# Attention beside a scan: score and value products as separate steps, the negated maxima turned by one product and carried to their rows by DMA

## Chip, core and metric

The kernel runs on one core of a Trainium2 chip. The metric is the device time of one execution in microseconds (us); for the kernel before it is the median of three runs. A profile is one more execution, recorded by the hardware; it gives every instruction's engine, line, start and duration. The engines: PE (TensorE, matrix products; PEld its weight loads), DVE (VectorE), ACT (ScalarE), POOL (GpSimd), SP (SyncE, which issues the DMAs). [...]

## What is computed

An input x of 16 images, 256 channels, 32 × 32 positions, float32, goes through two layers, each added to its own input. Layer 0 is attention over the 1024 positions of an image (4 heads of 32), layer 1 a selective state-space scan along the same 1024 positions (512 channels with 64 states each). Cut to what matters here:

```python
# layer 0, after group norm, position embedding and layer norm
q, k, v = (qkv[:, :, 0], qkv[:, :, 1], qkv[:, :, 2])
dots = jnp.einsum('bihd,bjhd->bhij', q, k) * scale
attn = jax.nn.softmax(dots, axis=-1)
out = jnp.einsum('bhij,bjhd->bihd', attn, v)
...
# layer 1
dA = jnp.exp(d_t[..., None] * A)
h = dA * h + (d_t * u_t)[..., None] * B_t[:, None, :]
y = jnp.einsum('bdn,bn->bd', h, C_t)
```

## The kernel before

**The scan sets the frame.** 512 channels × 64 states × 1024 positions of an image are cut into 256 *units*: 2 halves in time (t), 4 blocks of 128 channels (k), 4 quarters (q), 8 pairs of tiles (i). A unit is two tiles of 128 × 512. In the main loop (L927) each unit n does, in this order:

- `load(n + 6)` (L814): SP issues a DMA of 512 KB, the tile `dub`; there are seven buffers, so it waits until the scan of unit n − 1 has read its own;
- `inputs(n + 4)` (L824): POOL multiplies that tile twice in place;
- `scan(n)` (L846): DVE runs two scans over `dub` and the decays `a`;
- `decay(n + 2)`: PE makes two tiles `a` in PSUM (L833; four buffers, freed by `scan(n)`), ACT takes the exponential of each (L836);
- the *side work*: steps of another image's other stages, see below;
- a step of `outputs` (L870): the products of the states with C. A block of eight units has four halves of 16 output products on PE (L883), in the phases n mod 8 = 0, 1, 3, 4; after the second and fourth, ACT copies the sum away (`y`, L891) and in phases 2 and 5 PE turns it (L895); then ACT copies `yo` (L903) and SP stores it in phase 6 (L909).

**Side work is metered.** While the units of image b run, the other stages of image b + 1 (normalization, attention, the scan's inputs) and the last one of image b − 1 (gate and store) are produced by Python generators. Each `yield w` ends a step and says its weight w. Before the run, the weights of one image are summed; the loop (L951) adds `rate` per unit to `due` and takes steps until `due` is spent. So the steps of an image are spread over its units by weight, and a step's instructions stand in each engine's queue between `decay(n + 2)` and the `outputs` of that unit. At the end (L978) the program order is fixed by hand for PE, ACT, DVE and POOL; SP's queue follows the order of issue closely.

The first image's attention runs ahead of the first scan, the other fifteen beside the scans of the image before. The last image's scans have no attention beside them.

**Attention** (`attention_layer`, L324) takes two heads at a time, a *pair*, e = 0, 1 within it:

- `query_key(pair)` (L355): four steps; products into PSUM, then ACT copies 32 rows each to `qa` and `ka`. The head e has partitions 64e to 64e + 31; partition 64e + 32 of `ka` is set to ones by a small DMA (L358), and that of `qa` will take the negated maximum, so that one product of 33 rows gives score minus maximum;
- maxima: 16 steps (weight 1.1) of two score products each (L400), reduced by DVE in the next step (L391);
- rows: DVE negates the maxima into `neg`, with positions on partitions (L405). To bring them into one row, PE multiplies each of 16 columns by the identity (L412), a row of 128 each, and ACT copies four rows of 512 into `qa` (L415); two steps of 1.2;
- values: for each half of 512 query positions, eight steps of weight 1.5. Step j makes the two scores of key block j (L436), the value products of block j − 1 (L424), and the exponentials of j (L444), which free the two score buffers. One more step multiplies the last block and evacuates: ACT copies `ao` and `sums` of a head from the one PSUM accumulator `av` (L381, L382); the other head's copies follow in the next half's first step, or in a step of their own after the second half.

PSUM for all side work is a pool of two buffers (`mm`, L92).

Of the kernel before, what the change touches and what calls it, by code (L numbers as in the profile page):

```python
# [11 lines left out]
F32 = mybir.dt.float32  # L12
BF16 = mybir.dt.bfloat16
AF = mybir.ActivationFunctionType
# [5 lines left out]
P = 128  # L20
# [3 lines left out]
HL = 512  # L24
# [3 lines left out]
NJ = L // P  # L28
DI = 512
ND = DI // P  # L30
NS = 64
# [17 lines left out]
NV = _n  # L49
# [3 lines left out]
def attention_then_scan_kernel(  # L53
# [18 lines left out]
    nc = tc.nc  # L72
# [5 lines left out]
    const = pool("const", 1)  # L78
# [3 lines left out]
    ptp = pool("ptp", 4)  # L82
    small = pool("small", 2)
# [10 lines left out]
    def psum(name, dims=P):  # L94
        return mm.tile([P, HL], F32, name=name, tag="mm")[:dims]
# [7 lines left out]
    def hs(h):  # L103
        return ts(h, HL)


    vec = const.tile([P, NV], F32, name="vec")
    nc.sync.dma_start(vec, vecs)

    def col(name, i=0, n=1):  # L110
        o, w = _COLS[name]
        assert i + n <= w
        return vec[:, o + i : o + i + n]
# [5 lines left out]
    ident = const.tile([P, P], F32, name="ident")  # L119
# [13 lines left out]


    a_neg = work("a_neg", ND * NS)
    nc.scalar.activation(a_neg, col("A_log", 0, ND * NS), AF.Exp)
    nc.vector.tensor_scalar(a_neg, a_neg, -1.0, None, ALU.mult)
    acol = const.tile([P, DI // 2], F32, name="acol")
    a2 = work("a2", 2 * P).rearrange("p (j n i) -> p j n i", j=2, i=2)
    for k in range(ND):  # L140
# [4 lines left out]
        for j in range(2):  # L145
# [3 lines left out]
                start=(j == 0), stop=(j == 1),  # L149
# [22 lines left out]
    t = work("ones_s")[:1]  # L172
# [151 lines left out]
    def attention_layer(b):  # L324
# [54 lines left out]
        def evacuate(pair, hf, e):  # L379
            h, o = 2 * pair + e, 2 * DH * e  # L380
            nc.scalar.copy(ao[ts(h, DH), hs(hf)], av[o : o + DH])  # L381
            nc.scalar.copy(sums[ts(h, DH), hs(hf)], av[o + DH : o + 2 * DH])  # L382

        for pair in range(HEADS // 2):
            qa, ka = yield from query_key(pair)
            mx = small.tile([P, 2, NJ, 2], F32, name="mx", tag="mx")
            waiting = []

            def maxima():
                for s, e, c, hf in waiting:  # L390
                    nc.vector.tensor_reduce(mx[:, e, c, hf : hf + 1], s, AX.X, ALU.max)  # L391
                waiting.clear()

            for c in range(NJ):
                for hf in range(2):
                    maxima()
                    for e in range(2):
                        r = ds(2 * DH * e, DH)
                        s = psum("s_ps")
                        nc.tensor.matmul(s, qa[r, ts(c, P)], ka[r, hs(hf)], start=True, stop=True)  # L400
                        waiting.append((s, e, c, hf))
                    yield 1.1
            maxima()
            neg = small.tile([P, 2, NJ], F32, name="neg", tag="neg")
            nc.vector.tensor_reduce(neg, mx, AX.X, ALU.max, negate=True)  # L405
            for e in range(2):
                o = 2 * DH * e + DH
                for hf in range(2):
                    row = psum("row_ps", 1)
                    for c in range(NJ // 2):  # L410
                        i = hf * (NJ // 2) + c
                        nc.tensor.matmul(  # L412
                            row[:, ts(c, P)], neg[:, e, i : i + 1], ident, start=True, stop=True
                        )
                    nc.scalar.copy(qa[o : o + 1, hs(hf)], row)  # L415
                yield 1.2
            if pair == 0:
                ao, sums = work("ao"), work("sums")
            for hf in range(2):
                pts = []  # L420

                def values(j):
                    for e in range(2):
                        nc.tensor.matmul(  # L424
                            av[ts(e, 2 * DH)],
                            vv[j // (NJ // 2)][:, j % (NJ // 2), 2 * pair + e, :], pts[e],
                            start=(j == 0), stop=(j == NJ - 1),
                        )
                    pts.clear()

                for j in range(NJ):
                    scores = []
                    for e in range(2):
                        r = ds(2 * DH * e, DH + 1)
                        s = psum("st_ps")
                        nc.tensor.matmul(s, ka[r, ts(j, P)], qa[r, hs(hf)], start=True, stop=True)  # L436
                        scores.append(s)
                    if j == 1:
                        av = accp.tile([P, HL], F32, name="av", tag="av")
                    if pts:  # L440
                        values(j - 1)
                    for s in scores:
                        pt = ptp.tile([P, HL], F32, name="pt", tag="pt")
                        nc.scalar.activation(pt, s, AF.Exp)  # L444
                        pts.append(pt)
                    if j == 0 and hf == 1:
                        evacuate(pair, 0, 1)
                    yield 1.5
                values(NJ - 1)
                evacuate(pair, hf, 0)  # L450
                yield 1
            evacuate(pair, 1, 1)
            yield 1
# [584 lines left out]
```

## Time and profile before

| what | value |
|---|---|
| median of 3 runs | 13837.73 us |
| lowest and highest run | 13811.08 and 13840.92 us |
| the profiled execution | 13864.42 us |
| its span, first to last instruction | 13862.6 us |
| mean granted TensorE clock | 0.727 |
| DMA | 2804.18 MB, mean 202 GB/s |
| one scan (L846), 128 × 512 | 1203 ns in an image's first half, 1263 ns in its second |
| one product of a tile on POOL (L824) | 1302 ns |
| one exponential of the decay (L836) | 660 ns |
| one exponential of scores (L444) | 608 ns |
| one copy of a row of 512 (L415) | 573 ns, 128 of them |
| one instruction of the row products (L412) | 336 ns, 1024 of them |

How to read it: the page gives busy time by engine, then groups of instructions with their mean duration and the idle time before them. Float32 products appear as two instructions each, and their ends are modelled, so their durations overlap: the distance between starts is the better measure of what PE needs. A stretch of the run can be taken alone: "windows" list, for a stretch given by its start and end, its length, then busy time and count for PE, PEld, DVE, ACT and POOL, then the granted clock, the DMA engines' busy share and GB/s. "Timeline" lists instructions in order of time (start, length, engine, line, operation, tiles, count), with the idle time before one in brackets.

### The profile page before, as it was taken

Reading aid. Unit: us, or ns where it says so; the run is one execution under the profiler, and the core shown is the slowest. Engines: PE = TensorE matmul, PEld = TensorE weight load, DVE = VectorE, ACT = ScalarE, POOL = GpSimd, SP = SyncE. Lnnn points to the kernel's source line nnn. Section 1 sums busy time; section 2 is a strip of 40 time slices with the busy share of each in tenths; the row PEclk is TensorE's granted clock in tenths of the full one; section 3 lists DMA queues with packets and bytes.
Section 4 is the critical chain, followed back from the end, with each engine's and each line's share of the span. In section 5 each row is a group of like instructions: output and inputs, shape, how many; then the busy total and the mean of one; then the engine's idle time right before and its main releaser. Section 6 shows DMA issues by size and latency. Waiting matters only on the chain. (4 is left out here: it accounts for less than half of the span.)

```text
span 13862.6 us, 435096 instructions
## 1 busy us (share of the span) xinstructions
PE 11218.2 (81%) x185744; PEld 5762.9 (42%) x185744; DVE 12145.4 (88%) x11699; ACT 8103.3 (58%) x14245; POOL 10462.1 (75%) x8214
## 2 busy tenths in 40 slices
PE   7787977879788797887878878797787978879767
PEld 2344444444444444443444444444444444444434
DVE  2799888898989889888898888989898898988999
ACT  2565665656655566555665656566565665556544
POOL 0588777777787777777777777777777778777788
PEclk6776777767778677786777767677676777767767
DMA  1466566565665656656566665656666566565666
GB/s 38 166 207 226 187 201 220 197 229 182 204 221 196 229 179 214 211 197 224 194 210 206 201 217 199 220 193 202 220 200 228 185 206 223 193 230 183 213 215 225
DMA packets 964174, 2804.18 MB, mean 202 GB/s; under 512 B 138162, under 2 KB 285747, under 8 KB 962228
## 3 DMA queue, kind: packets, MB, share of 16 engines
q1 hardware_dynamic: 962228, 2776.34, 59.9%
q8 instruction: 1452, 23.79, 0.7%
q14 instruction: 494, 4.05, 0.1%
HBM read 2514.18 MB, written 261.62 MB: 200 GB/s over the span
## 5 line engine op out<-in xcount | busy, mean ns | idle before, releaser
L824 POOL TENSOR_TENSOR dub<-dub,bt 128x512 f32<-128x512 f32 x8192 | 10407.0, 1302 | 3350.8 <-DMA dub<-dus 2960.7
L836 ACT ACTIVATE a<-a,acol 128x512 f32<-128x512 f32 x8192 | 5066.9, 660 | 3844.0 <-PE a L833 3808.6
L846 DVE TENSOR_TENSOR_SCAN h<-a,last,dub 128x512 f32<-128x512 f32 x4096 | 4939.7, 1263 | 246.6 <-POOL dub L824 188.3
L846 DVE TENSOR_TENSOR_SCAN h<-a,dub 128x512 f32<-128x512 f32 x4096 | 4705.0, 1203 | 286.8 <-POOL dub L824 150.6
L833 PE MATMUL a<-pieces,pick 48*128 48x512 bf16 x8192 | 2915.2, 481 | 2261.8 <-DVE h L846 2215.0
L883 PEld LDWEIGHTS yb<-h,cd 128*32 128x32 f32 x131072 | 2685.0, 140 | 1992.8 <-issue 1725.0
L883 PE MATMUL yb<-h,cd 128*32 128x64 f32 x131072 | 3093.9, 266 | 26.1 <-issue 14.2
L833 PEld LDWEIGHTS <-pick 48*128 48x128 bf16 x8192 | 506.6, 96 | 2632.6 <-issue 2418.5
L400 PE MATMUL s_ps<-ka,qa 32*128 32x512 f32 x2048 | 1142.4, 1025 | 42.0 <-ACT ka L371 26.4
L391 DVE TENSOR_REDUCE mx<-s_ps 128x1 f32<-128x512 f32 x1024 | 656.9, 680 | 302.7 <-PE s_ps L400 301.3
L895 PEld LDWEIGHTS yb<-turn,y 128*16 128x16 f32 x32768 | 416.5, 120 | 1028.2 <-ACT y L891 409.0
L891 ACT COPY y<-yb 128x256 f32<-128x256 f32 x1024 | 383.7, 375 | 765.4 <-PE yb L883 762.9
L895 PE MATMUL yb<-turn,y 128*16 128x32 f32 x32768 | 552.3, 216 | 149.4 <-ACT y L891 139.2
L436 PE MATMUL st_ps<-qa,ka 33*128 33x512 f32 x2048 | 634.9, 654 | 2.6 <-ACT pt L444 2.5
L424 PE MATMUL av<-pt,vv 128*64 128x512 f32 x2048 | 613.0, 678 | 0.9
L444 ACT ACTIVATE pt<-st_ps 128x512 f32<-128x512 f32 x1024 | 559.3, 608 | 77.1 <-PE st_ps L436 75.5
L400 PEld LDWEIGHTS s_ps<-ka,qa 32*128 32x128 f32 x2048 | 350.1, 277 | 429.7 <-DVE mx L391 237.2
L618 PE MATMUL g_ps<-w,xp 128*128 128x256 f32 x1536 | 453.6, 451 | 0.0
L618 PEld LDWEIGHTS g_ps<-w,xp 128*128 128x128 f32 x1536 | 391.1, 328 | 102.5 <-issue 63.3
L603 DVE SCALAR_TENSOR_TENSOR u<-up,cwh,u 128x1024 f32<-128x1024 f32 x192 | 304.4, 1585 | 27.4 <-ACT u L595 27.1
L771 PE MATMUL m_ps<-w,xs 128*128 128x256 f32 x1024 | 316.2, 458 | 10.5 <-DVE xs L746 10.5
L771 PEld LDWEIGHTS m_ps<-w,xs 128*128 128x128 f32 x1024 | 261.3, 328 | 90.2 <-issue 59.4
(135 smaller groups left out, 7581.0 us busy)
## 6 DMA issues: line engine op xcount, KB each, us to landing
dub<-dus SPq DMA_DIRECT2D x4096, 512.0 KB
dps<-pc SPq DMA_DIRECT2D x384, 128.0 KB
pieces<-dps SPq DMA_DIRECT2D x1024, 48.0 KB
xs<-in_x_dram SPq DMA_DIRECT2D x64, 512.0 KB
xs<-kept SPq DMA_DIRECT2D x64, 512.0 KB
zs<-z SPq DMA_DIRECT2D x64, 512.0 KB
ud<-u SPq DMA_DIRECT2D x64, 512.0 KB
dus<-du SPq DMA_DIRECT2D x64, 512.0 KB
```

The source lines that it names most:

```text
L391: nc.vector.tensor_reduce(mx[:, e, c, hf : hf + 1], s, AX.X, ALU.max)
L400: nc.tensor.matmul(s, qa[r, ts(c, P)], ka[r, hs(hf)], start=True, stop=True)
L424: nc.tensor.matmul(av[ts(e, 2 * DH)], vv[j // (NJ // 2)][:, j % (NJ // 2), 2 * pair + e, :], pts[e], start=(j == 0), stop=(j == NJ - 1),)
L436: nc.tensor.matmul(s, ka[r, ts(j, P)], qa[r, hs(hf)], start=True, stop=True)
L618: nc.tensor.matmul(ps[:, ts(q, C)], xp[k][:, ds(first + t, P, 4)], wg_s[:, k, t, :], start=(i == 0), stop=False,)
L771: nc.tensor.matmul(ps[:, ts(q, C)], us[d][:, ds(first, P, 4)], wo_s[:, d, :], start=(d == 0), stop=(d == ND - 1),)
L824: nc.gpsimd.tensor_tensor(v, v, blocks[b, t]["bt"], ALU.mult)
L833: nc.tensor.matmul(a, w, pieces[r], start=True, stop=True)
L836: nc.scalar.activation(a, a, AF.Exp, scale=acol[:, at : at + 1])
L846: nc.vector.tensor_tensor_scan(now["h", q % 2][:, 2 * i + e, :], decays[n][e], loaded[n][:, e, :], first, ALU.mult, ALU.add,)
L883: nc.tensor.matmul(yb[ts(g, 32), ts(s, 64)], cd[:, at // 16, ts(c, 32)], hbuf[:, :, at : at + 4], start=(c == 0), stop=(c == 3),)
L895: nc.tensor.matmul(out4[32 * s : 32 * s + 16, half, e], y2[:, 64 * s + e : 64 * s + 64 : 4], turn[:, e], start=True, stop=True,)
```

## The change

Inside attention:

- `query_key(0)` is made ahead of the loop over pairs, and `query_key(1)` in pair 0 after its rows, in place of the start of pair 1. In pair 1 two steps without instructions stand there.
- The 16 row products of a pair become one: `neg` with its 16 columns is the stationary operand, the identity moves; the result has 16 rows of 128. ACT copies it to a small tile `few`, 16 × 128, in one instruction. SP then issues two DMAs, each of which takes eight rows of 128 to the one row of 1024 in `qa`.
- A values step of 1.5 becomes a score step of 0.8 (two score products and their two exponentials) and a values step of 0.8 (the value products of the block before). Order on each engine is as before, scores of j ahead of values of j − 1.
- The weights of an image's attention fall from 112.8 to 112.0.
- To make room for `few`, the last columns of the vector constants (A_log) are no longer kept; they are fetched by a DMA of their own into a work tile at the start.

```diff
-    vec = const.tile([P, NV], F32, name="vec")
-    nc.sync.dma_start(vec, vecs)
+    NC = NV - ND * NS
+    vec = const.tile([P, NC], F32, name="vec")
+    nc.sync.dma_start(vec, vecs[:, :NC])
...
     a_neg = work("a_neg", ND * NS)
-    nc.scalar.activation(a_neg, col("A_log", 0, ND * NS), AF.Exp)
+    nc.sync.dma_start(a_neg, vecs[:, NC:])
+    nc.scalar.activation(a_neg, a_neg, AF.Exp)
...
+        ahead = yield from query_key(0)
         for pair in range(HEADS // 2):
-            qa, ka = yield from query_key(pair)
+            qa, ka = ahead
...
             nc.vector.tensor_reduce(neg, mx, AX.X, ALU.max, negate=True)
+            turned = psum("row_ps", 2 * NJ)[:, :P]
+            nc.tensor.matmul(
+                turned, neg.rearrange("p e c -> p (e c)"), ident, start=True, stop=True
+            )
+            few = small.tile([2 * NJ, P], F32, name="rows", tag="rows")
+            nc.scalar.copy(few, turned)
+            yield 1
             for e in range(2):
                 o = 2 * DH * e + DH
-                for hf in range(2):
-                    row = psum("row_ps", 1)
-                    for c in range(NJ // 2):
-                        i = hf * (NJ // 2) + c
-                        nc.tensor.matmul(
-                            row[:, ts(c, P)], neg[:, e, i : i + 1], ident, start=True, stop=True
-                        )
-                    nc.scalar.copy(qa[o : o + 1, hs(hf)], row)
-                yield 1.2
+                nc.sync.dma_start(
+                    qa[o : o + 1].rearrange("p (c t) -> p c t", c=NJ), few[ts(e, NJ)]
+                )
+            if pair == 0:
+                ahead = yield from query_key(1)
+            else:
+                yield 1
+                yield 1
...
                 for j in range(NJ):
-                    scores = []
+                    made = []
                     for e in range(2):
                         r = ds(2 * DH * e, DH + 1)
                         s = psum("st_ps")
                         nc.tensor.matmul(s, ka[r, ts(j, P)], qa[r, hs(hf)], start=True, stop=True)
-                        scores.append(s)
+                        pt = ptp.tile([P, HL], F32, name="pt", tag="pt")
+                        nc.scalar.activation(pt, s, AF.Exp)
+                        made.append(pt)
+                    if j == 0 and hf == 1:
+                        evacuate(pair, 0, 1)
+                    yield 0.8
                     if j == 1:
                         av = accp.tile([P, HL], F32, name="av", tag="av")
                     if pts:
                         values(j - 1)
-                    for s in scores:
-                        pt = ptp.tile([P, HL], F32, name="pt", tag="pt")
-                        nc.scalar.activation(pt, s, AF.Exp)
-                        pts.append(pt)
-                    if j == 0 and hf == 1:
-                        evacuate(pair, 0, 1)
-                    yield 1.5
+                        yield 0.8
+                    pts.extend(made)
                 values(NJ - 1)
                 evacuate(pair, hf, 0)
                 yield 1
```

## The prediction, on record before the result was known

> **What bounds the kernel now.** I read the busy times first. VectorE (DVE) is the fullest engine; the others have room on average.
>
> ```profile
> PE 11218.2 (81%) x185744; PEld 5762.9 (42%) x185744; DVE 12145.4 (88%) x11699; ACT 8103.3 (58%) x14245; POOL 10462.1 (75%) x8214
> ```
>
> An average says nothing of the attention stage, so next I took windows over it, in all 15 images whose attention lies beside a scan. The first set runs from pair 0's negated maxima (L405) to pair 1's first maximum: rows, values, then the projections of pair 1. The second runs from pair 1's L405 to its last evacuation. In both DVE has nothing to do but scans. Two images of each, and the sum over 15:
>
> ```profile
> 6612.60:6693.80 81.20, 76.18 (x1465) 36.17 (x1458) 71.13 (x63) 68.50 (x129) 72.87 (x60) 0.94 0.62 213
> 7458.80:7540.50 81.70, 76.55 (x1465) 36.11 (x1456) 71.10 (x63) 68.65 (x129) 72.35 (x59) 0.94 0.64 213
> sum 1225.80, PE 1149.98 PEld 544.89 DVE 1072.52 ACT 1030.29 POOL 1091.66; mean PE 76.67 PEld 36.33 DVE 71.50 ACT 68.69 POOL 72.78
> ...
> 4209.50:4278.10 68.60, 64.18 (x1301) 30.74 (x1302) 62.56 (x56) 58.94 (x115) 62.00 (x51) 0.97 0.62 209
> 6751.80:6826.10 74.30, 69.96 (x1278) 32.14 (x1282) 62.77 (x56) 59.49 (x115) 63.57 (x52) 0.87 0.59 193
> sum 1094.80, PE 1023.88 PEld 473.50 DVE 945.25 ACT 892.86 POOL 946.74; mean PE 68.26 PEld 31.57 DVE 63.02 ACT 59.52 POOL 63.12
> ```
>
> The third busy column is DVE, the last but two the TensorE clock. DVE idles 1225.8 − 1072.5 = 153.3 us and 1094.8 − 945.3 = 149.5 us: 302.8 us, **20.2 us an image**. This is all that the change can win beside the scans. See too that pair 1 takes 68.6 us where the clock was 0.97 and 74.3 where it was 0.87, for the same work.
>
> Who ends this idle time? The table of waits says POOL, wrongly: matching the n-th multiplication to the n-th scan, POOL was done 6 us ahead or more in these stages, whereas the decay's exponential ended 0.1 us before a scan that had waited. So it is the chain PE decay (L833), ACT exponential (L836), scan. One unit's PE work, in time order:
>
> ```profile
> 6661.29 0.39 PE L833 MATMUL a<-pieces,pick 48*128 48x512 bf16 x2
> 6661.52 1.02 PE L436 MATMUL st_ps<-qa,ka 33*128 33x512 f32 x4
> 6662.47 1.08 PE L424 MATMUL av<-pt,vv 128*64 128x512 f32 x4
> 6663.48 1.10 PE L883 MATMUL yb<-h,cd 128*32 128x64 f32 x64
> 6664.51 0.39 PE L833 MATMUL a<-pieces,pick 48*128 48x512 bf16 x2
> ```
>
> By starts: decay 0.23, scores 0.95, values 1.01, half of an output 1.03, in all 3.22 us, while DVE's two scans take 2.25 (2.37 in an image's second half). And at pair 1's change of halves:
>
> ```profile
> 6789.04 0.58 ACT L382 COPY sums<-av 32x512 f32<-32x512 f32 x1
> 6789.64 0.37 ACT L891 COPY y<-yb 128x256 f32<-128x256 f32 x1
> 6790.07 0.63 PE L895 MATMUL yb<-turn,y 128*16 128x32 f32 x32 [1.91 <-ACT y L891]
> 6790.63 0.61 PE L833 MATMUL a<-pieces,pick 48*128 48x512 bf16 x2
> 6790.67 2.34 DVE L846 TENSOR_TENSOR_SCAN h<-a,dub 128x512 f32<-128x512 f32 x2 [1.49 <-POOL dub L824]
> ```
>
> and windows over the four units about it and the four after:
>
> ```profile
> 6781.80:6792.90 11.10, 9.19 (x220) 4.35 (x218) 9.24 (x8) 10.30 (x19) 11.10 (x10) 0.87 0.67 211
> 6792.90:6808.00 15.10, 15.10 (x170) 5.08 (x172) 9.75 (x10) 8.96 (x18) 12.91 (x11) 0.64 0.46 156
> ```
>
> PE sits 1.91 us behind ACT's evacuation copies, its decay then lasts 0.61 instead of 0.39, and the next four units take 15.1 us (clock 0.64) where DVE needs 9.75.
>
> [...] maxima stages show 0.50, full values stages 1.00, and the dip follows a pause. [...] Here SP issued den at 6826.15 and the dependent few at 6829.99: 3.84 us a hop under load.
>
> **The change, part by part.** A unit is two scans; the image has 256, and the rate is (249.8 + 26.6)/247 = 1.119 of step weight a unit, afterwards 1.116, so steps outside attention shift by at most a unit: nothing, ±2 us an image.
>
> *Values in steps of their own.* A joint step (1.5) becomes 0.8 + 0.8. I placed the steps on the units and kept a backlog: PE's work of a unit (0.23 + scores + values + output phase: 1.03, 1.03, 0.40, 1.03, 1.03, 0.40, 0, 0) less 2.25 or 2.37; what exceeds 1.0 us stalls DVE, since exponentials end about 1.0 us early when nothing waits. (In the first image's period the rate is 1.011; taken alike.) PE's work by unit:
>
> ```
> before, 65-94:   3.0 2.4 2.2 3.2 .6 2.2 2.2 3.2 1.3 2.6 3.2 3.2 .6 1.2 1.2 3.2 3.2 .6 3.2 3.2 2.6 .2 2.2 3.2 2.3 .6 2.2 1.3 1.6 .2
> after, 65-94:    1.5 1.6 1.3 2.2 .6 2.1 1.2 3.2 2.2 1.6 3.2 2.2 2.6 1.2 1.2 3.3 2.2 1.6 3.2 2.3 1.6 2.2 1.2 3.2 2.2 1.6 3.2 2.3 .6 .2
> before, 110-136: .2 2.0 3.0 2.2 2.6 3.2 1.3 2.6 2.2 2.2 1.3 3.2 2.6 2.3 2.2 .6 2.2 2.2 3.2 1.3 2.6 3.2 3.2 .6 2.2 1.2 1.3
> after, 110-136:  .5 .2 2.2 2.2 2.6 2.3 2.2 2.6 1.2 2.2 2.2 2.3 2.6 2.3 2.2 2.6 1.2 2.2 2.3 2.2 2.6 2.3 2.2 2.6 1.2 1.2 1.3
> ```
>
> Before: joint steps next to output halves (units 75 and 76, 80 and 81, 83 and 84, 131 and 132, 0.97 over each) and the rows give 4.3 + 2.4 us; ACT in the same way (decay 1.16, pair of exponentials 1.0, evacuation 1.15) 1.0 + 0.6. After: in pair 1 no unit exceeds 2.59, PE 1.2 + 0, ACT 1.5 + 0.7 (two score steps in one unit at pair 0's start; evacuations stay). Saved: 8.3 − 3.4 = **4.9 us an image**.
>
> *The clock.* The backlog explains 8.3 of 20.2. Much of the rest is half clock: ten of fifteen pair-1 windows at 0.86 to 0.88 lose 74.3 − 68.6 = 5.7 us, one at 0.91 about 2; mean 3.9. Afterwards, in that unit, scores and values stand ahead of the turn that waits for y, so PE has work in the pause: I take 3.9 saved. In pair 0 the like block took 12.3 us for 9.0 (clock 0.86); half of 3.3, **1.6**. Bounds for both: 0 and 7.2.
>
> *Rows.* 32 products (16 a pair) and 8 copies go (an image's rows were 1024/16 = 64 instructions of PE, 0.11 us apart when warm, 7.0 us, and 8 × 0.573 = 4.6 us of ACT); two products of 16 columns and two copies of 128 (between the 0.22 of 16 columns and 0.375 of 256) come. DVE idled 2.9 us in units 67 to 71 and 2.5 in 112 to 118, of which the backlog holds 1.9 (0.8 and 1.0); I add **2** for the rest, bounds 0 and 3.5.
>
> *Transfers.* PE's product waits for L405 as before. Behind the SP wait for the copy stand the next dub loads (L814): in pair 1 one leaves 3.1 us late, POOL's lead is then 18 us; uncovered, 3.1 us an image. Pair 0's rows have four units, 9 us, to land. Pair 1's: copy done about 0.7 us into unit 111, both issued by 1.7, landing 2 to 3.8 later; scores of unit 112 reach PE at about 4.75. Late by 0 to 0.8; behind them on PE stand an output half and the decay of unit 115, and for that waits DVE. Unit 111 has no side work, so PE comes in at half clock. Together **−1.0**, bounds 0 and −3.
>
> *Projections in the gap.* Same four steps, moved from units 91–94 to 66–69, with their two ones loads on SP (0.44 us each, under the same lead). ACT 2.3 us a unit, at DVE's pace there as here: 0. But pair 1's maxima then follow a light unit instead of dense products, and were 57–58 us after a warm start, 61.8 cold: mean 59.2; I take **−0.5**, bound −2.6.
>
> *A_log's own load* and the smaller vec: start only, 0 to +1 us, 0 taken.
>
> Sum: 4.9 + 3.9 + 1.6 + 2 − 1.0 − 0.5 = 10.9 us × 15 = 164. In the first image, before any scan, the rows took 6.6 us a pair (L405 at 114.5, first scores 121.1): perhaps 6 saved of both. **170 us**. The profiled execution took 13864.4 (span 13862.6): 13694 after. It lies 0.2% above the median of the runs, 13837.7; the same difference gives 13668.
>
> **Rivals.** *Only the rows count* (chance 0.17): ACT's copies still set the pause and the dips stay, so 4.9/2 + 2 − 1.5 = 3 us × 15 + 6 = 51: 13787. For it: evacuations are unchanged. Against: S and V now precede the waiting turn. *Nearly all idle time goes* (0.13): 17 × 15 + 6 = 261: 13577. Beyond that POOL is next: its pair takes 2.45 to 2.5 us, DVE 2.25, and the 6 us of lead left are eaten at 0.25 a unit over 25 units. *The clock falls* (0.12, slower): split steps and the empty unit leave PE at half clock in a values stage. Price: 15.1 − 9.75 = 5.35 us per four units. It decides from two such blocks more than today an image (10.7 against 10.9); with three, 5.2 × 15 = 78 lost: 13916. For it: at half clock scores and values alone did not wake the clock for 12 us. Against: pair 1's units 112 and 113 carry output halves, after which it rose.
>
> **How the numbers follow.** Forecast 13668 with 0.58. To be told from no change takes 0.2%, 28 us. Faster 0.83 (forecast, full gain, most of rows only), same 0.07, slower 0.10. Range 13580 to 13835: from the full gain to just short of no change; it leaves out the falling clock and about 0.06 more.
>
> **What would show it.** Right: pair-1 windows all near 68 us at clock 0.97, pair 0 near 74; DVE idle in the two sets near 9 us an image; scans in unit 112 on time. Wrong: clock under 0.9 in values windows, PE waiting there for the row DMA, POOL's multiplication ending just before the scan, or maxima of pair 1 all at 62 us.

## The result and the profile after

The changed kernel takes **13883.2 us** (median; 13870.3 to 13904.9), the kernel before 13837.2 in the same comparison: ratio **1.0039**, 95% interval 1.0021 to 1.0057. Its median is 46 us longer, the mean of its runs 53; I had forecast 170 us less, and the time lies outside my range. The profiled execution of after took 13870.3 us (span 13868.5), the lowest of its runs, while that of before lay 27 us above its median; so the two traces differ by 6 us only, and show the places rather than the whole sum. In the changed kernel the scan is L855, its decay L842 with the exponential L845, the score product L445 with its exponential L447, the values L433.

The busy times of the page, columns as before, tell nothing of it:

```profile
PE 11127.7 (80%) x184784; PEld 5684.2 (41%) x184784; DVE 12142.3 (88%) x11699; ACT 8024.2 (58%) x14149; POOL 10449.7 (75%) x8214
```

Windows over the same two stages as in the prediction (from the negated maxima of pair 0 to the first maximum of pair 1; from those of pair 1 to its last evacuation), one of each, beside the scans of the eighth image (called image 8 from here), and the sum over 15:

```profile
6611.40:6691.60 80.20, 74.75 (x1439) 33.65 (x1432) 69.04 (x62) 64.78 (x123) 68.72 (x57) 0.91 0.64 222
sum 1230.80, PE 1150.72 PEld 519.87 DVE 1044.35 ACT 975.96 POOL 1049.40; mean PE 76.71 PEld 34.66 DVE 69.62 ACT 65.06 POOL 69.96
...
6751.30:6823.10 71.80, 66.34 (x1252) 29.93 (x1256) 64.51 (x58) 58.34 (x116) 63.92 (x52) 0.89 0.61 209
sum 1076.70, PE 990.35 PEld 447.75 DVE 973.18 ACT 878.03 POOL 974.25; mean PE 66.02 PEld 29.85 DVE 64.88 ACT 58.54 POOL 64.95
```

DVE's idle time in them is 1230.8 − 1044.4 = 186.4 and 1076.7 − 973.2 = 103.5: 19.3 us an image, where it was 20.2 in the kernel before. Pair 1 gained, pair 0 lost. To see where, I cut each image at the scans of fixed units and took means over 13 images (the 3rd to the 15th), in us. The last five columns are experiments, told below:

| units, what runs there | before | after | E1 weight back | E6 split alone | E7 rest alone | E13 before, 64 rows | E9 after, 64 rows |
|---|---|---|---|---|---|---|---|
| 46–65, pair 0's maxima | 71.2 | 70.5 | 70.9 | 70.1 | 71.2 | 65.6 | 65.6 |
| 65–70, its rows | 14.8 | 13.5 | 13.5 | 14.4 | 13.5 | 13.5 | 12.8 |
| **70–80, its first values** | 25.7 | **31.3** | 31.2 | 24.5 | 31.1 | 25.7 | 28.0 |
| 80–94 | 37.2 | 35.6 | 35.7 | 36.3 | 38.1 | 36.7 | 34.6 |
| 94–112, pair 1's maxima | 66.5 | 64.8 | 65.1 | 66.2 | 65.5 | 61.9 | 60.0 |
| **112–122, its first values** | 25.4 | 27.3 | 26.8 | **28.4** | 25.8 | 25.6 | 25.4 |
| 126–134, its change of halves | 24.7 | **20.4** | 20.4 | 20.7 | 22.8 | 21.5 | 20.4 |
| 122–126 and 134–142 | 35.9 | 34.5 | 34.4 | 35.2 | 35.7 | 36.3 | 34.8 |
| **142–206, later steps** | 221.7 | **226.8** | 221.7 | 223.2 | 222.2 | 222.2 | 222.2 |
| whole image | 846.8 | 847.3 | 843.1 | 843.1 | 849.7 | 833.1 | 827.6 |

How far such means repeat, E2 tells (below): its attention is that of before, on the same units. There these stretches differ from the column "before" by 0.5 us at most, pair 0's maxima by 1.3.

Attention, down to unit 142, gained 3.5 us an image; the steps behind it lost 5.1. Inside attention one dip of the clock went and another came. Windows of image 8, units 68 to 72, 72 to 76 and 76 to 80 of pair 0; then units 112 to 116 of pair 1; then 124 to 128 and 128 to 132, about its change of halves, which had been 11.10 and 15.10 us before:

```profile
6616.00:6626.10 10.10, 8.53 (x209) 4.25 (x208) 9.19 (x10) 9.68 (x18) 8.48 (x8) 0.99 0.69 238
6626.10:6642.20 16.10, 15.37 (x161) 6.11 (x160) 9.38 (x9) 9.53 (x19) 13.88 (x12) 0.58 0.38 142
6642.20:6652.60 10.40, 10.40 (x230) 4.82 (x230) 9.19 (x8) 8.32 (x17) 6.46 (x6) 1.00 0.57 196
6753.60:6765.60 12.00, 10.77 (x145) 5.36 (x146) 9.13 (x9) 7.10 (x14) 8.59 (x7) 0.50 0.59 193
6785.70:6796.40 10.70, 10.38 (x224) 4.95 (x222) 9.15 (x9) 10.20 (x20) 9.34 (x9) 1.00 0.69 245
6796.40:6805.80 9.40, 9.40 (x161) 3.87 (x158) 9.38 (x8) 8.58 (x17) 9.40 (x8) 1.00 0.61 204
```

See the clock (last but two): the block that had taken 15.1 us runs at 1.00 and takes 9.4. But four units at pair 0's start now take 16.1 us at 0.58. This is how TensorE got there (timeline, start and duration, in brackets its idle time and who ended it):

```profile
6621.58 0.39 PE L842 MATMUL a<-pieces,pick 48*128 48x512 bf16 x2
6622.75 0.47 PE L904 MATMUL yb<-turn,y 128*16 128x32 f32 x32 [0.78 <-ACT y L900]
6623.15 0.39 PE L842 MATMUL a<-pieces,pick 48*128 48x512 bf16 x2
6623.38 1.02 PE L445 MATMUL st_ps<-qa,ka 33*128 33x512 f32 x2
6625.09 1.32 PE L445 MATMUL st_ps<-qa,ka 33*128 33x512 f32 x2 [0.69 <-ACT ka L373]
6627.14 2.56 PE L445 MATMUL st_ps<-qa,ka 33*128 33x512 f32 x4 [0.73 <-ACT pt L447]
6629.01 1.12 PE L842 MATMUL a<-pieces,pick 48*128 48x512 bf16 x2
```

Three pauses behind ACT, none over 0.8 us. The clock record falls at 6625.9, between the second and the third. The next two scores together (x4) take 2.56 us, where they took 1.02 in the kernel before (L436 in the prediction), and the next decay, behind them, comes late and lasts 1.12 us. ACT copies the projections out (L370, L373: 0.59 and 0.58 us each) in just these units, and the second pause ends with such a copy.

The waits name the other loss (us in all, times, longest):

```profile
DVE xp L259 <- ACT gn_v_ps L256: 41.1, 16, 3.8
...
DVE ao L485 <- DMA sums<-den: 29.8, 11, 5.7
```

Before, the second was 12.7 (its line is L476 there), and the first is 8.2, as it is again when the later steps stand at their old units (E1); in E2, the kernel before with these steps shifted, they are 41.1 and 42.8. A step that waits for a transfer or for ACT meets DVE one unit earlier, and DVE stands still.

### The profile page after: what moved, and what is told of

Its sections match the earlier page's. It is cut to its first block, busy times and chain, and to the rows that moved or that the text cites. A ratio compares the mean times of both kernels' runs of the same rounds, so it can differ in the third digit from the quotient of the medians.

```text
span 13868.5 us, 433154 instructions
## 1 busy us (share of the span) xinstructions
PE 11127.7 (80%) x184784; PEld 5684.2 (41%) x184784; DVE 12142.3 (88%) x11699; ACT 8024.2 (58%) x14149; POOL 10449.7 (75%) x8214
## 5 line engine op out<-in xcount | busy, mean ns | idle before, releaser
L845 ACT ACTIVATE a<-a,acol 128x512 f32<-128x512 f32 x8192 | 5071.2, 662 | 3921.5 <-PE a L842 3885.5
L855 DVE TENSOR_TENSOR_SCAN h<-a,last,dub 128x512 f32<-128x512 f32 x4096 | 4932.9, 1261 | 170.0 <-POOL dub L833 103.5
L855 DVE TENSOR_TENSOR_SCAN h<-a,dub 128x512 f32<-128x512 f32 x4096 | 4701.7, 1201 | 326.0 <-POOL dub L833 218.5
L842 PE MATMUL a<-pieces,pick 48*128 48x512 bf16 x8192 | 2936.1, 481 | 2294.0 <-DVE h L855 2265.2
L842 PEld LDWEIGHTS <-pick 48*128 48x128 bf16 x8192 | 515.3, 97 | 2623.8 <-issue 2421.2
L403 PE MATMUL s_ps<-ka,qa 32*128 32x512 f32 x2048 | 1103.2, 998 | 37.7 <-DVE mx L394 35.5
L445 PE MATMUL st_ps<-qa,ka 33*128 33x512 f32 x2048 | 699.8, 698 | 22.5 <-ACT ka L373 11.6
L447 ACT ACTIVATE pt<-st_ps 128x512 f32<-128x512 f32 x1024 | 561.4, 606 | 179.4 <-PE st_ps L445 176.1
L433 PE MATMUL av<-pt,vv 128*64 128x512 f32 x2048 | 624.2, 695 | 0.9
L627 PEld LDWEIGHTS g_ps<-w,xp 128*128 128x128 f32 x1536 | 396.4, 329 | 116.3 <-issue 65.5
L445 PEld LDWEIGHTS st_ps<-qa,ka 33*128 33x128 f32 x2048 | 239.9, 210 | 264.8 <-ACT pt L447 119.9
```

The source lines that it names most:

```text
L433: nc.tensor.matmul(av[ts(e, 2 * DH)], vv[j // (NJ // 2)][:, j % (NJ // 2), 2 * pair + e, :], pts[e], start=(j == 0), stop=(j == NJ - 1),)
L627: nc.tensor.matmul(ps[:, ts(q, C)], xp[k][:, ds(first + t, P, 4)], wg_s[:, k, t, :], start=(i == 0), stop=False,)
L842: nc.tensor.matmul(a, w, pieces[r], start=True, stop=True)
L845: nc.scalar.activation(a, a, AF.Exp, scale=acol[:, at : at + 1])
L855: nc.vector.tensor_tensor_scan(now["h", q % 2][:, 2 * i + e, :], decays[n][e], loaded[n][:, e, :], first, ALU.mult, ALU.add,)
```

## Experiments

Each ratio is to the kernel before, run on the same chip at the same time.

### E1 and E2: the weight alone

E1 is the changed kernel with the 0.8 of weight that its attention lost put back at its end; E2 is the kernel before with 0.8 taken off there. In both the rate is split at unit 137, so that attention keeps the units of its own kernel. The diff is E1's; E2 has `yield 0.2` and `total + 0.8` in the same places.

```diff
             evacuate(pair, 1, 1)
-            yield 1
+            yield 1.8 if pair else 1
...
-            rate, due = total / (UNITS - AHEAD - 3), 0.0
+            later = total / (UNITS - AHEAD - 3)
+            rate, due = later, 0.0
+            if b + 1 < B:
+                rate = (total - 0.8) / (UNITS - AHEAD - 3)
...
+            if at == 137:
+                due, rate = due + 137 * (later - rate), later
```

> The changed kernel with its attention on the same units, but with the 0.8 of weight that attention had lost put back behind it, so that every step from unit 137 on stands where it stood before the change. Theory A (the displaced steps cost: units 142 to 206 took 5.1 us an image longer in the profile after than in the one before): 14 images x 5.1 = 71 us faster than the changed kernel, 13883 - 71 = 13812, a ratio of 0.998 to the kernel before, and the 14 stretches of units 142 to 206 back from about 227 to 221 us. Theory B (a step a unit earlier or later costs nothing, the loss lies inside attention): no change, 13883, ratio 1.003.

> The kernel before, its attention untouched and on the same units, but with 0.8 less weight behind it, so that every step from unit 137 on stands where the changed kernel has it. Theory A: 71 us slower than the kernel before, 13908, ratio 1.005, with 'ao' waiting for its DMA in unit 142 and the second group norm waiting for ACT in unit 169 as in the profile after. Theory B: as the kernel before, ratio 1.000 within 0.001.

E1: **0.9998** (0.9988 to 1.0008); units 142 to 206 take 221.7 us again. E2: **1.0036** (1.0023 to 1.0048); they take 226.9. Shown in both directions: 0.36 to 0.41% of the time is lost by the position of steps that the change doesn't touch. With that set aside, the change is worth nothing, and the question is where 170 us went.

### E3: the first two score steps apart

The changed kernel, with pair 0's second score step moved from unit 70 to 71.

```diff
-                    yield 0.8
+                    yield {0: 1.3, 1: 0.3}.get(j, 0.8) if (pair, hf) == (0, 0) else 0.8
```

> The changed kernel with one step moved: pair 0's second score step stands in unit 71 instead of unit 70, where the first one stands too; all other steps are on their units. Theory A (two score steps in one unit make PE wait twice for ACT, its clock falls to one half, and units 70 to 80 take 31.4 us for 25.6): units 70 to 80 near 25.5 us, 15 x 5.6 = 84 us faster than the changed kernel, 13799, ratio 0.997. Theory B (the separate steps cost by themselves, wherever they stand): less than 15 us of it comes back, ratio 1.002 or more.

**1.0039** (1.0025 to 1.0053), units 70 to 80 at 31.1. My theory fell: two score steps in one unit are not the cause, the stall moved by a unit and stayed.

### E4: products in pair 1's empty steps

The changed kernel; two unused products of 128 rows in each of the two empty steps.

```diff
-                yield 1
-                yield 1
+                for _ in range(2):
+                    ps = psum("warm_ps")
+                    for k in range(KC):
+                        nc.tensor.matmul(
+                            ps, wqk_s[:, k, ts(pair, P)], xn[k][:, hs(_)],
+                            start=(k == 0), stop=(k == KC - 1),
+                        )
+                    yield 1
```

> The changed kernel with work added: in the two empty steps of pair 1 PE makes four dense products of 128 x 512 (the projections of pair 1 once more, not used by anything). Theory A (PE enters pair 1's values at half clock after the empty unit, and units 114 to 118 pay for it): the clock of units 112 to 116 rises from 0.50 to 0.8 or more, units 112 to 122 fall from 27.7 to about 25 us, 15 x 2.7 = 40 us faster than the changed kernel, 13843, ratio 1.000. Theory B (the slow start is the row's DMA or ACT, not the clock): added work on PE brings nothing or 1 to 2 us an image more, ratio 1.003 to 1.006.

**1.0019** (1.0012 to 1.0025). The interval overlaps with that of the changed kernel, so the total alone shows little; the stage is clear. Units 112 to 122 went from 27.3 to 25.7, and in image 8 the window of units 112 to 116, which had been 12.00 us at clock 0.50, is now:

```profile
6727.84:6737.90 10.06, 10.06 (x155) 4.42 (x153) 9.12 (x10) 6.76 (x14) 6.74 (x6) 0.92 0.62 192
```

More work in the gap made the stage behind it shorter: TensorE's clock (0.50 in the changed kernel, 0.92 here), and not its work, is what pair 1's first values lack in the changed kernel.

### E5: products ahead of pair 0's first scores

E1 with a 256-column unused product ahead of each of the first four scores.

```diff
                         s = psum("st_ps")
+                        if (pair, hf) == (0, 0) and j < 2:
+                            nc.tensor.matmul(
+                                s[:, : HL // 2], wqk_s[:, e, ts(1, P)], xn[e][:, : HL // 2],
+                                start=True, stop=True,
+                            )
```

> The change, with the later steps at the units they had before (as in the run that put the weight back, ratio 0.9998), and with one unused product (128 rows, 256 columns) ahead of each of the four scores of pair 0's first two score steps: TensorE does 1.9 us more an image. Theory (TensorE does too little in units 70 to 72, waiting for ACT's copies of the projections, so its clock falls to half just after, in units 72 to 76): units 70 to 80 fall from 31.3 to 26 or 27 us, the image by about 4.5, the run to about 13790, ratio 0.995. Rival (the half clock comes from the 33-row scores and 64-column values themselves, whatever stands before them): units 70 to 80 stay at 31 or grow by what the products take, ratio 1.000 to 1.002.

**1.0026** (1.0015 to 1.0037), units 70 to 80 at 33.9: a miss. The timeline of image 8 offers a reason:

```profile
6654.98 0.47 PE L909 MATMUL yb<-turn,y 128*16 128x32 f32 x32 [1.26 <-ACT y L905]
...
6655.70 0.70 PE L446 MATMUL st_ps<-xn,w 128*128 128x256 f32 x2
6656.33 1.95 PE L450 MATMUL st_ps<-qa,ka 33*128 33x512 f32 x2
6658.21 1.22 PE L446 MATMUL st_ps<-xn,w 128*128 128x256 f32 x2
```

The first product (L446) took 0.70, the second 1.22, the score between them 1.95: the clock fell while they ran (0.84 over units 70 and 71 in this image, 0.50 over the 13.1 us of the two behind them). They came behind a pause of 1.26 us, and then stood ahead of a decay that took 0.61 for 0.39. On record this is the rival's outcome, 31 us and what the products take (1.9), and a little more; the reading by the timeline came afterwards. The run speaks against filling at that place and leaves open which of the two is right.

### E6 and E7: each half of the change alone

E6 is the kernel before with the split of scores and values alone (the loop over j as in the change; the weights sum to the same). E7 is E1 with that loop as before, with its joint step of 1.5: turned rows, transfers and projections in the gap. The core of E6's diff:

```diff
+                        pt = ptp.tile([P, HL], F32, name="pt", tag="pt")
+                        nc.scalar.activation(pt, s, AF.Exp)
+                        made.append(pt)
...
+                    yield 0.8
                     if j == 1:
                         av = accp.tile([P, HL], F32, name="av", tag="av")
                     if pts:
                         values(j - 1)
...
-                    yield 1.5
+                        yield 0.8
```

> The kernel before with one part of the change alone: scores and values in steps of their own. Rows by 32 products and eight copies, and the projections between the pairs, as before; the sum of the weights is that of before, so later steps stay where they were. Theory (the dip at pair 0's start comes from the projections in the gap, the one at pair 1's start from the empty units; the split is good by itself): units 70 to 80 near 25.7 or less, 112 to 122 near 25, 126 to 134 at 20.4 instead of 24.7; about 6 us an image, 13770, ratio 0.9935. Rival (the split itself starves TensorE at pair 0's start): units 70 to 80 at 31, so that the image wins nothing, ratio 0.999 to 1.001.

> The complement: rows turned by one product and brought by transfers, projections of pair 1 in the gap, but scores and values joint in one step of 1.5 as before; later steps at the units they had before. Theory: units 70 to 80 near 31 (half clock after the light units), 112 to 122 at 27 or more, 126 to 134 back at 24.7, 65 to 70 at 13.5; so 5 us an image slower than before, 13930, ratio 1.005. Rival (the split is what starves TensorE): units 70 to 80 at 25.7 or less, ratio 0.999 to 1.001.

E6: **0.9949** (0.9934 to 0.9964). E7: **1.0051** (1.0033 to 1.0069). Their product is 1.0000, and E1, which has both, 0.9998: the change is a gain of half a per cent and a loss of half a per cent. Pair 0's dip goes with the rows and the projections in the gap, which E7 moves together, and not with the split: four units of image 8 from unit 72, E6 (two windows) and E7 (two windows):

```profile
6596.00:6600.50 4.50, 4.31 (x70) 1.66 (x70) 4.50 (x5) 4.34 (x9) 4.25 (x4) 1.00 0.64 205
6600.50:6604.90 4.40, 4.40 (x105) 2.01 (x94) 4.40 (x5) 3.51 (x9) 4.13 (x4) 1.00 0.61 233
```

```profile
6659.00:6665.90 6.90, 6.19 (x17) 1.84 (x14) 4.56 (x4) 4.58 (x9) 6.90 (x6) 0.59 0.69 226
6665.90:6674.00 8.10, 8.10 (x148) 3.62 (x144) 4.62 (x5) 4.73 (x10) 6.36 (x7) 0.72 0.27 93
```

Two expectations failed. The change of halves took 22.8 us in E7, where I had expected the old 24.7: part of that gain comes without the split. And I had put the slow start of pair 1 down to the empty steps alone. But E6 has none and takes 28.4 there, E7 has them and takes 25.8. E6 loses it in one unit, 115 (5.6 us for 2.4, mean of the 13 images), and its trace shows how (image 8; in E6 the score is L436, its exponential L438):

```profile
6722.13 0.39 PE L833 MATMUL a<-pieces,pick 48*128 48x512 bf16 x2
6722.35 1.02 PE L436 MATMUL st_ps<-qa,ka 33*128 33x512 f32 x4
6724.39 1.61 PE L436 MATMUL st_ps<-qa,ka 33*128 33x512 f32 x4 [1.01 <-ACT pt L438]
6725.93 1.77 PE L883 MATMUL yb<-h,cd 128*32 128x64 f32 x64
6727.64 0.61 PE L833 MATMUL a<-pieces,pick 48*128 48x512 bf16 x2
```

Two score steps fall into one unit; the second waits 1.01 us for the exponentials that free its buffers, and from decay to decay go 5.5 us. The clock is not the main cause: its mean over units 112 to 122 is 0.92 in the kernel before, 0.88 in E6 and 0.83 in E7, and in E10, below, unit 115 runs at 1.00 and still takes 4.85 us. In the changed kernel these two steps lie in units of their own. What pair 1's start loses there is the clock (0.53 over units 112 to 116, before 0.81), and E4, with 0.92 in image 8, shows that this goes back to the empty steps.

### What the clock follows

In the traces of before and after the clock record has two values, 0.50 and 1.00, and all but its last stretch are multiples of 3.41 us. I cut both into these 8095 windows and asked of each: how much of it TensorE was busy, and what the clock was in the next. Busy time decides little: of 1747 full windows at half clock (busy over 0.99) 762 were followed by full clock, 985 by half. Then I weighted TensorE's time with an estimate of mine, from the rows that the trace lists for each product, over 128, the most that any of them has: outputs, values, projections 1; the two heads' scores or maxima side by side (2 × 33, 2 × 32 rows, starts under 0.01 us apart) 0.5; decays (48) 0.375; products of 16 rows 0.25 (the last from a fit). The decays don't follow from the rows alone: two of them start together as well, which would make 0.75, but then about twice as many windows at full clock lie on the wrong side (123 instead of 62 of 3646). Windows by that sum, as "next at half / next at full":

```
weighted share     0-.4     .4-.5    .5-.6    .6-.7    .7-.8    .8-.9    .9 up
at full clock    593/0    224/48   27/225    2/419    0/554    0/543    0/1011
at half clock   1270/0     473/0    401/0   1012/0   417/158   24/223    8/463
```

At full clock 817 of the 865 windows with a share below 0.5 were followed by half clock, and 29 of the 2781 above it; at half clock 686 of the 718 windows above 0.8 were followed by full clock, and 158 of the 3731 below it. Parted at 0.48 and 0.80, 62 and 190 windows, some 3%, lie on the wrong side. In the window before pair 0's dip of image 8 (from 6622.5) TensorE was busy 0.72 of the time, 0.53 with scores: weighted 0.41. In the four half-clock windows that follow it is 0.38, 0.74, 0.78, 0.76. Before pair 1's old dip (from 6786.7) it was 0.36; after, in the same place (6789.7), 0.65, since scores fill the pause. This was still an ordering of the records of two traces, with weights chosen to fit. The next runs test it.

### E8, E9, E10: the same products over 64 rows

Rows 33 to 63 of each head hold zeros, brought by transfers, so the scores are unchanged; so is the number of columns. E8 is E1 with the scores so, E9 with the maxima too, E10 is E6 with both. The last line for r is that of the scores, the one ahead of it that of the maxima, which E8 leaves alone.

```diff
-    ones = dram1.tile([1, L], F32, name="ones", tag="ones")
-    t = work("ones_s")[:1]
-    nc.vector.memset(t, 1.0)
+    ones = dram1.tile([2 * DH, L], F32, name="ones", tag="ones")
+    t = work("ones_s")[: 2 * DH]
+    nc.vector.memset(t, 0.0)
+    nc.vector.memset(t[:1], 1.0)
...
-                nc.sync.dma_start(ka[2 * DH * e + DH : 2 * DH * e + DH + 1], ones)
+                r = ds(2 * DH * e + DH, DH)
+                nc.sync.dma_start(ka[r], ones[:DH])
+                nc.sync.dma_start(qa[r], ones[DH:])
...
-                        r = ds(2 * DH * e, DH)
+                        r = ds(2 * DH * e, 2 * DH)
...
-                        r = ds(2 * DH * e, DH + 1)
+                        r = ds(2 * DH * e, 2 * DH)
```

> The change with the later steps at their old units (its time 0.9998 of before), and the products of the scores run over 64 rows a head instead of 33: the 31 rows more hold zeros, brought by transfers, so the sums are the same and so is the number of columns. Theory, from the clock records and TensorE's work in their windows of 3.41 us in four traces: the clock falls after a window in which time times the share of the 128 rows in use is below about 0.48, and rises after one above about 0.80; two products of 33 rows side by side count a half. With 64 rows they count whole: the half clock in units 72 to 76 ends two windows sooner, that of units 112 to 117 one. Units 70 to 80 from 31.2 to about 28.4, 112 to 122 from 26.8 to 25.6; about 4 us an image, 13795, ratio 0.9955. Rival (only TensorE's busy time counts, or the count of its instructions): no stage moves, and the transfers cost a little; ratio 1.000 to 1.002.

> The same, and the products of the maxima over 64 rows too (row 32 and those behind it hold zeros in one factor until the row of minus the maxima comes). Theory: the maxima, which ran at half clock for most of two times 20 units, have windows above 0.80 now and rise; at full clock they come to about 0.50, so they fall again now and then. Idle time of VectorE in units 46 to 65 from 9.6 to about 5, in 94 to 112 from 5.1 to about 3: 6 to 7 us an image more than with the scores alone; ratio 0.988. Rival (rows don't count): units 46 to 65 stay at 71, ratio 1.000 to 1.002.

> The kernel before with the split steps alone (ratio 0.9949), and all products of scores and maxima over 64 rows. Theory: units 112 to 122 from 28.4 to about 26, 46 to 65 from 70.1 to about 66, 94 to 112 from 66.2 to about 62: 10 us an image less than the split alone, 13620, ratio 0.983. Rival (rows don't count): 0.995 to 0.997, as the split alone.

E8: **0.9909** (0.9891 to 0.9928); units 70 to 80 at 28.9, 112 to 122 at 25.4, as expected. E9: **0.977** (0.9751 to 0.9789). E10: **0.9813** (0.9795 to 0.983); its units 46 to 65 take 65.6 and 94 to 112 take 62.1, as expected, but 112 to 122 still 27.2. Filling up the rows of some products with zeros is worth 2.3%: the rival, for which only busy time counts, is out, and that the rows in use count is shown for these products. The weights are still a fit. Four units of pair 0's maxima in image 8, after and then E9:

```profile
6588.70:6604.40 15.70, 15.70 (x185) 7.23 (x186) 13.92 (x17) 6.07 (x11) 9.12 (x9) 0.50 0.37 135
```

```profile
6389.20:6402.90 13.70, 11.70 (x185) 5.07 (x184) 13.70 (x17) 5.71 (x12) 10.19 (x9) 1.00 0.64 205
```

The same 185 instructions, clock 0.50 and 1.00; TensorE busy throughout and DVE idle 1.8 us, then DVE without a gap. I had expected 0.9955 and 0.988. The surplus is partly ahead of the first scan, where the first image's attention runs alone: it begins at 484.0 us in after, 445.7 in E8, 419.1 in E9. That part I hadn't counted. What remains inexact: with 64 rows the windows fit best with a weight between a half and one.

### E11, E12, E14: projections back, with 64 rows

E11 is E9 with pair 1's projections back between the pairs, and one empty step ahead of pair 0's scores. E12 puts unused products (two a step, as in E4) into its three empty steps. E14 has two empty steps in both pairs. The weights sum to those of before in each; the rate of E1 is taken out. The core of E11's diff, against the changed kernel (E14 has its second `yield 1` in both pairs and 0.4 at their ends):

```diff
-            if pair == 0:
-                ahead = yield from query_key(1)
-            else:
-                yield 1
+            yield 1
+            if pair == 1:
                 yield 1
...
-            yield 1
+            yield 0.8 if pair else 1
+            if pair == 0:
+                ahead = yield from query_key(1)
```

> The run with all products over 64 rows (ratio 0.977), with the projections of pair 1 back between the pairs, and one empty step between pair 0's row transfers and its scores. Theory A (the projections in the gap load ACT in units 66 to 70, TensorE waits behind it, and the clock falls for pair 0's first values): units 70 to 80 from 28.0 to about 25, the rest as there; 13490, ratio 0.974. Theory B (any gap without rows to turn leaves TensorE light, as in pair 1's empty units): units 70 to 80 stay at 27 to 28, ratio 0.977. For both, 94 to 112 stays near 60 to 61.

> As the run beside it, with two unused products (128 rows, 512 columns) in each of the three empty steps, one step ahead of pair 0's scores and two ahead of pair 1's. By A and by B the clock is kept into the values: units 112 to 122 from 25.4 to about 24.5, and by B also 70 to 80 to about 25; 13475 to 13490, ratio 0.973 to 0.974. If the work itself costs time: 0.975 or more.

> As the run with 64 rows and the projections back between the pairs (ratio 0.981), with two empty steps ahead of pair 0's scores, as pair 1 has. If what it lost was TensorE's wait for the row transfers (2.75 us of PE's idle in image 7, scores beginning 3 us late): units 65 to 80 from 42.4 to about 38, ratio 0.975. If a second empty step drops the clock instead, as in pair 1's entry: units 70 to 80 at 26 to 27 and ratio 0.979 to 0.981.

E11: **0.9808** (0.9789 to 0.9827), slower than E9; I had expected 0.974. In image 8 the clock is 1.00 from unit 70 to 80, and these units take 24.7 us (28.0 in E9), as theory A had it. But units 65 to 70 went from 12.8 to 17.7, and the half clock has only moved ahead: its record lies from 6459.0 to 6465.8, before unit 70 (6466.9). TensorE now waits for the rows, which the projections had hidden. Timeline of SP's queue, then of TensorE, in E11:

```profile
6453.94 1.53 SPq L421 DMA_DIRECT2D qa<-rows  x2
```

```profile
6458.70 2.25 PE L446 MATMUL st_ps<-qa,ka 64*128 64x512 f32 x4 [2.75 <-DMA qa<-rows]
```

From the start of the issue to the first score, 4.8 us: two units. The wait is not all that E11 lost: units 65 to 80 explain 1.6 of the 5.5 us that its images take more than E9's (833.1 and 827.6), the maxima of pair 1 another 2.2 (62.2 and 60.0), which no run explains. With two empty steps (E14) units 65 to 80 fall from 42.4 to 38.5, as expected. But units 70 to 80 went from 24.7 to 25.9, and the whole run, **0.9813** (0.9798 to 0.9827) and not 0.975, can't be told from E11's; it stays inconclusive. E12: **0.9813** (0.9794 to 0.9832), where I had expected 0.973 to 0.974. In pair 0 the filling paid: units 65 to 80 took 39.9 us for 42.4. In pair 1 the clock record went to 1.00 a window sooner, but the products held TensorE for 5.7 us, and units 112 to 122 went from 24.3 to 26.6. The two cancel.

### E13: the kernel before, with 64 rows

The diff of E8 with both lines for r, on the kernel before.

> The kernel before, nothing of the change in it, with the products of scores and maxima over 64 rows a head. By the theory of rows in use: units 46 to 65 from 71.2 to 65.6, 94 to 112 from 66.5 to about 62, 126 to 134 from 24.7 to about 22 (its dip ends sooner), and 30 us at the start: about 0.983. It tells what the whole change is worth once the clock is held: against 0.977 for the change with 64 rows, the change is then worth 0.6%, the size of the stalls and not of the clock. If the change is worth nothing without the clock: 0.977 to 0.979 here.

**0.9819** (0.9805 to 0.9832), as expected. Against E9's 0.977 the change, with the clock mostly held and the later steps in place, is worth about 0.5%. The two traces differ by 92 us (E13's is the slowest of its runs, 19 us above its median): 30 ahead of the first scan (449.6 and 419.1), 72 beside the scans of the first fifteen images, and the last image gives 10 back. The 30 us go with the clock. The first image's maxima of pair 0, E9 and then E13:

```profile
74.10:105.70 31.60, 27.89 (x64) 9.37 (x64) 20.03 (x31) 2.26 (x4) 0.00 (x0) 1.00 0.00 1
73.80:120.60 46.80, 43.12 (x64) 15.66 (x64) 20.06 (x31) 2.32 (x4) 0.00 (x0) 0.52 0.00 0
```

Those of pair 1 took 30.3 and 45.2 us. In E11, whose program is E9's down to the end of pair 0's maxima, pair 0's took 45.3 us at 0.55; so pair 0's share is not the work of the change. In the same way the first scan begins at 480.6 us in before and at 466.1 in E2, with one program ahead of it.

Set beside E6 and E7, the parts have changed their signs. With 33 rows the split gained 0.51% and the rest lost as much; with 64 rows the split gains nothing that can be told from zero (E10 against E13, 0.9813 and 0.9819), and the rest gains 0.4% (E9 against E10), of which 27 us lie ahead of the first scan. E9 is the fastest kernel of the study.

## Why the prediction was wrong

**Steps outside attention: nothing, ±2 us an image.** This step failed: +5.1. I had worked out that they shift by at most a unit, and took a shift for free. A step that ends on a wait has a price for its unit: `ao` met the transfers of `den` one unit earlier (29.8 us of waiting in all for 12.7), the group norm's product its ACT step at once (41.1 for 8.2). E1 and E2 show it from both sides.

**Projections in the gap: "ACT 2.3 us a unit, at DVE's pace: 0".** This failed too: 5.6 us in units 70 to 80, 5.4 in E7 (E6 doesn't have it). ACT's sum was about right: in units 68 to 72 of image 8 it is busy 9.68 us, 2.4 a unit, DVE 9.19. But TensorE stands behind ACT for 0.9 us of one clock window whose work is mostly scores, and the clock falls (0.50 from 6625.9 to 6639.6). I had looked for pauses of the old kind, one long wait; none here is over 0.8 us. E7 doesn't separate the projections from the row products that are gone; E11 and E12, which do, have 64 rows: without the projections in the gap units 70 to 80 are back at 24.7 and 24.3 us. That it is the light window, and not something else in these units, is argued from the clock record and supported by E8 (28.9), not shown alone.

**Values in steps of their own, with the clock: 4.9 + 3.9 + 1.6.** The split alone gave 0.51% of 13861, 71 us, 4.7 an image instead of 10.4. The mechanism at the change of halves was right, and so was its price: 24.7 to 20.7 (E6) or 20.4 (after), against 3.9. Pair 0's start and the units to 94 gave another 2.1 in E6. E7 has 1.9 of the 4.3 without the split. What took the split's gain back in E6 is pair 1's start, +3.0, the unit with two score steps; I had reckoned with such a unit only at the changed kernel's pair 0.

**Rows: 2.** Units 65 to 70 gave 1.3; right in kind. **Transfers and the entry at half clock: −1.0.** In after, image 8, pair 1's scores start on time (transfers issued from 6752.69, scores from 6756.10, no wait ahead of them), so the transfers cost nothing as placed. My 3.84 us a hop was an upper limit (in before it took 1.94 us in the first image, ahead of the scans): the load of `few` stood in SP's queue behind a load of `dub` that was issued from 6829.39 to 6829.90. E11 shows the uncovered price of the rows, 2.75 us of waiting. The entry at half clock is real, +1.9 in units 112 to 122, and E4 takes 1.6 of it away by filling the empty steps. With joint steps a like clock (0.58 over units 112 to 116 in E7) costs 0.4. **Maxima of pair 1: −0.5.** Wrong in sign, a gain of 1.7 (1.0 in E7): I had taken the start's clock as the thing that counts; what made the gain, no run shows. **The first image: 6 us.** Not seen: the first scan begins at 484.0 us, before at 480.6, and between the kernel before and E2, which have one program there, it moves by 14.5 us.

**Rivals.** "The clock falls", which I gave 0.12, named the thing: scores without values at half clock in a values stage. Its price of 5.35 us for four such units was near: units 70 to 80 lost 5.6. But it expected this from the split and the empty unit, where in pair 0 it came with the rows and projections (E7) and not with the split (E6); and without the displaced later steps its time would have been wrong as well, since E1 is at 0.9998.

## What to carry to other kernels

Read TensorE's clock from the trace and not from its busy time (in image 8 four units of E9's maxima ran at 1.00, where in after TensorE was busy throughout the same four and ran at 0.50): sum its work over windows of the clock record, weighted by the rows in use (here a fitted weight), and look at every place where a change puts narrow products next to waits. If a narrow product takes no more time with more rows (one score instruction took 654 ns on average in before, over 33 rows, and 648 in E9, over 64), zeros in the rows are worth trying; here they brought 2.3%, more than the rearrangement. And when weights of a planner change, the steps that are not part of the change move too: hold them in place first, then measure.

## What was not expected of the hardware

- Being busy throughout a window of 3.41 us didn't by itself raise TensorE's clock: 985 of 1747 full windows at half clock were followed by another at half clock, 976 of them with a weighted share under 0.8 (by my fitted weights).
- The clock fell from 1.00 to 0.50 after a window in which TensorE was busy 0.72 of the time, with no pause over 0.8 us (after, image 8, from 6622.5).
- Scores and maxima over 64 rows instead of 33 or 32, with the same columns, brought the clock of four units of maxima from 0.50 to 1.00 (after and E9, image 8), and their time from 15.7 to 13.7 us.
